# Cross-attention and feed-forward block: three output weights in the projection weights' buffers, attention results fetched one head group ahead, and the first pair's last output group recorded inside the second pair

## The chip, the core and the metric

The kernel runs on one core of one Trainium2 chip. The metric is the device time of one execution in microseconds (us); of each kernel several executions are timed, and the median stands for it. Beside these, one execution was taken with the hardware profiler; every view of the profile comes from that one. Engines are called as in the profile: PE (TensorE), DVE (VectorE), ACT (ScalarE), POOL (GpSimd), SP (SyncE, which here only issues transfers).

## What is computed

Eight sequences `x` of 128 tokens by 512 features, eight contexts `ctx` of the same size, float32 throughout. Cut to what matters, the reference is

```
n   = layernorm(x)
h   = rmsnorm(n) * ln_weight
q   = h @ w_q.T;  k = ctx @ w_k.T;  v = ctx @ w_v.T        # 32 heads of 128
p   = softmax(q k.T + position_bias, where mask else -inf)  # per head, 128 x 128
att = p @ v                                                # 128 x 4096
x1  = x + n + att @ w_out.T                                # 4096 -> 512
f   = layernorm(x1)
out = x1 + ((silu(f @ Wg.T * ag) * (f @ Wu.T * au)) @ Wd.T) * ad   # 512 -> 1376 -> 512
```

The change lies in the part from `p` to `x1`.

## The kernel before

**Products in seven.** The large products (q, k, v, output, gate and up) are cut into two by two blocks and made from seven block products instead of eight, with sums of blocks before and after. The sums of a weight's blocks are four instructions on POOL (`sums_a`, L191, for the projections; `sums_b`, L199, for the output weights). The sums of the attention results are four on DVE (`sums_a`, called in `attended`, L450). Their outputs go to a tile of sums beside the weight or result, and one block of the operand itself is overwritten.

**Stages.** The 32 heads are eight groups of four (g), the eight sequences four pairs (i).
1. Keys and values of group 0, the first norms, then the queries of all groups, which are stored in DRAM.
2. The loop over g (L491), inside it the loop over eight sequences b (L510). For each b the scores of four heads (`probabilities`, L292), softmax, a transposition by way of DRAM (`transpose_p`, L331: a DVE transpose, one store `turned`, four loads `pT`), and, three steps later (`advance(3)`), the product with v (`attend`, L353), whose result goes to DRAM (`att[g][i]`). Between these steps the keys and values of group g + 1 are projected (`kv`, L371), three or four block products a step, each for one half of the outputs.
3. The output projection. `out_products(i, order, banks)` (L462) is a generator: for each group g it loads `att[g][i]` as tile `a` (L452), makes the sums S_a on DVE, and records 28 matmuls (fourteen in the source, each executed as two) into four PSUM banks. Each pair needs all eight groups. The first pair's banks are the projections' own (`first_banks`), so its groups are interleaved with the loop of g = 7, where no projection is left: one `next(first_out)` after each of b = 0 to 6, and the last after `advance(0)` (L528). Then come the residual and second norm of pair 0 (`residual`, L536, `norm2`, L557), and the pairs 1 to 3 with all their products (L582 on).
4. Feed-forward, in the end the down projection (L712).

**Output weights.** `load_wo(g)` (L443) loads 1 MB and records four POOL sums into T_o. Weights 0 and 1 have buffers of their own (`wosA`) and are loaded at g = 1 and 2. Weights 2 to 6 get buffers (`wosB`, five) in the place of the context tile `toks`, which the projections read to their end: the pools `toks`, `spool` (sums of projection weights, two buffers) and `wpool` (projection weights, three buffers) are closed together at g = 7 (L502). Weight 7 uses activation buffers and is loaded after the loop.

**What sets the order.** The source gives each instruction its engine and its priority by the place where it is recorded. A scheduler then orders each engine's instructions, assigns buffers and adds the waits. On the chip each engine's queue is taken in that order: an instruction that waits holds up all that stand behind it, also the transfers on SP, which loads `wo`, `a`, `q`, `pT` and stores `turned` and `att`. POOL has, besides the weight sums, the sum of bias and mask for each step (L296), which the softmax needs; three such tiles `s` are in turn. Scores have two PSUM banks, attends two, and `acts` holds eighteen tiles for k, v, q, a and S_a together.

Of the kernel before, what the change touches and what calls it, by code (L numbers as in the profile page):

```python
# [9 lines left out]
F32 = mybir.dt.float32  # L10
# [4 lines left out]
PSUM = bass.MemoryType.PSUM  # L15

P = 128
# [8 lines left out]
def xattn_ffn_kernel(  # L26
# [20 lines left out]
    B, S, D = x.shape  # L47
    H = pbias.shape[0]
    INTER = wgT.shape[1]
    T = B * S  # L50
    DC = D // P
    GH = 4
    NG = H // GH
# [5 lines left out]
    HC = DC // 2  # L59
    HW = GW // 2  # L60
    ADD, SUB = ALU.add, ALU.subtract

    def pools(stack):
        def pool(name, bufs=1, **kw):
            return stack.enter_context(tc.tile_pool(name=name, bufs=bufs, **kw))
        return pool
# [6 lines left out]
    work = pool("work", 2, side="right", reuse_waits="tile")  # L73
    small = pool("small", 4, side="right", reuse_waits="tile")

    proj, rows, attn = ExitStack(), ExitStack(), ExitStack()
    toks = pools(proj)("toks", reuse_waits="tile")
    spool = pools(proj)("spool", 2, reuse_waits="tile")
    wpool = pools(proj)("wpool", 3, reuse_waits="tile")
    hpool = pools(rows)("hpool", side="right", reuse_waits="tile")  # L80
    ps_mm, ps_tp, ps = (pools(attn)(f"ps{n}", 2, space=PSUM) for n in ("mm", "tp", "at"))

    def load_w(name, src):
        t = wpool.tile([P, DC, GW], F32, tag="w", name=name)
# [341 lines left out]
    outp = ExitStack()  # L426
# [3 lines left out]
    def load_wo(g):  # L430
        src = woT[bass.ts(g, GW), :].rearrange("(c p) n -> p c n", p=P)
        if g == NG - 1:
            up, dn, t12, t4 = (
                acts.tile([P, 2, D], F32, tag="a", name=f"wo{g}_{k}") for k in range(4)
            )
            nc.sync.dma_start(up, src[:, :HC])
            nc.sync.dma_start(dn, src[:, HC:])
            t1, t2, t4 = (
                t.rearrange("p (c n) -> p c n", c=HC) for t in (t12[:, 0], t12[:, 1], t4[:, 0])
            )  # L440
        else:
            w = wos.tile([P, GH, D], F32, tag="w", name=f"wo{g}")
            nc.sync.dma_start(w, src)  # L443
            t = wos.tile([P, 3, HC, HW], F32, tag="T", name=f"T_o{g}")
            up, dn, t1, t2, t4 = w[:, :HC], w[:, HC:], t[:, 0], t[:, 1], t[:, 2]
        wo_t[g] = sums_b(
            nc.gpsimd, up[:, :, :HW], up[:, :, HW:], dn[:, :, :HW], dn[:, :, HW:], t1, t2, t4
        )

    def attended(g, i):  # L450
        a = acts.tile([P, 2, GH, S], F32, tag="a", name=f"a_{g}_{i}")
        nc.sync.dma_start(a, att[g][i])  # L452
        s = acts.tile([P, 3, HC, S], F32, tag="a", name=f"S_a{g}_{i}")
        return sums_a(
            nc.vector, a[:, 0, :HC], a[:, 0, HC:], a[:, 1, :HC], a[:, 1, HC:],
            s[:, 0], s[:, 1], s[:, 2],
        )

    def by_product(banks):
        return {n: banks[k // 2][:, k % 2, :] for k, n in enumerate((1, 2, 6, 7, 4, 5, 3))}  # L460

    def out_products(i, order, banks):  # L462

        m = by_product(banks)
        for g in order:
            sa = attended(g, i)
            for k, n in enumerate((1, 2, 6, 7, 4, 5, 3)):
                for c in range(HC):
                    nc.tensor.matmul(  # L469
                        m[n], sa[n][:, c, :], wo_t[g][n][:, c, :],  # L470
                        start=(g == order[0] and c == 0 and k % 2 == 0),
                        stop=(g == order[-1] and c == HC - 1), skip_group_check=True,
                    )
            yield


    def load_bias(g):
# [13 lines left out]
    for g in range(NG):  # L491
        kT, v = kvs.pop(g)
        pb = biases.pop(g)
        if g + 1 < NG:
            biases[g + 1] = load_bias(g + 1)
        if g + 2 < NG:
            kv_w[g + 2] = load_kv(g + 2)
        products = kv(g + 1, kvs) if g + 1 < NG else iter(())
        if g in (1, 2):
            load_wo(g - 1)  # L500
        if g == NG - 1:
            proj.close()  # L502
            wos = pools(outp)("wosB", NG - 3, reuse_waits="tile")

            first_banks = [
                pl.tile([P, 2, HW], F32, tag=tag, name=f"m{k}_0")
                for k, (pl, tag) in enumerate(((ps_mm, "mm"), (ps_mm, "mm"), (ps_tp, "pt"), (ps_tp, "pt")))
            ]
            first_out = out_products(0, list(range(NG)), first_banks)
        for b in range(B):  # L510
            if b % 2 == 0:
                qT = ahead.pop((g, b // 2))
                at = todo.index((g, b // 2)) + 2
                if at < len(todo):
                    ahead[todo[at]] = load_queries(*todo[at])
            p = probabilities(g, b, qT, kT, pb)
            pend.append((g, b, transpose_p(g, b, p), v))
            advance(3)
            for _ in range(4 if b % 2 else 3):
                next(products, None)  # L520
            if g == NG - 1:
                if b < NG - 3:
                    load_wo(b + 2)
                if b < NG - 1:
                    next(first_out)
    load_wo(NG - 1)
    advance(0)
    next(first_out)  # L528
    attn.close()


# [4 lines left out]
    def residual(i, xs, m, banks):  # L536
        r1, r2 = xs[:, 0, :], xs[:, 1, :]
        u = work.tile([P, 2, HW], F32, tag="s", name=f"u_{i}", bufs=3)
        w = work.tile([P, HW], F32, tag="s", name=f"u7_{i}", bufs=3)
        nc.scalar.copy(u[:, 0], m[1])  # L540
        nc.vector.tensor_tensor(u[:, 1], u[:, 0], m[6], ADD)
        nc.vector.tensor_tensor(w, u[:, 1], m[7], ADD)
        nc.vector.tensor_tensor(r1[:, :HW], r1[:, :HW], m[2], ADD)
        nc.gpsimd.tensor_tensor(r1[:, :HW], r1[:, :HW], u[:, 0], ADD)
        nc.vector.tensor_tensor(r1[:, HW:], r1[:, HW:], m[5], ADD)
        nc.vector.tensor_tensor(r1[:, HW:], r1[:, HW:], m[3], ADD)
        nc.gpsimd.tensor_tensor(r1[:, HW:], r1[:, HW:], u[:, 1], ADD)
        nc.vector.tensor_tensor(r2, r2, banks[2][:].rearrange("p a n -> p (a n)"), ADD)
        nc.vector.tensor_tensor(
            r2.rearrange("p (a n) -> p a n", a=2), r2.rearrange("p (a n) -> p a n", a=2),  # L550
            w.unsqueeze(1).to_broadcast([P, 2, HW]), ADD,
        )
# [4 lines left out]
    def norm2(i, xs):  # L557
        for k in range(2):
            st = small.tile([P, nc.vector.BN_STATS_DIM], F32, tag="st", name=f"st2_{i}_{k}")
            moments(mv2, 2 * i + k, st, xs[:, k, :])  # L560
        pair = slice(2 * i, 2 * i + 2)
        rstd_of(rs2[:, pair], mv2[:, pair, 1], 1.0)
        ys = []
        for b in (2 * i, 2 * i + 1):
            y = work.tile([P, D], F32, tag="aT", name=f"y2_{b}")
            nc.vector.tensor_scalar(
                y, xs[:, b % 2, :], mv2[:, b, 0:1], rs2[:, b : b + 1], ALU.subtract, ALU.mult
            )
            ys.append((b, y))
        return ys  # L570

    def norm2_T(b, y):
        th, cols = b * S // 512, bass.ds(b * S % 512, S)
        if (0, th) not in h2:
            for f in range(2):
                h2[f, th] = acts.tile([P, HC, 512], F32, tag="a", name=f"h2_{f}_{th}")
        tp = transposed(y, ps.tile([P, DC, P], F32, tag="tp", name="tp2", bufs=1))
        nc.vector.tensor_copy(h2[0, th][:, :, cols], tp[:, :HC])
        nc.scalar.copy(h2[1, th][:, :, cols], tp[:, HC:])

    x1, ys, banks = [], [], first_banks
    for i in range(B // 2):  # L582
        last = i + 1 == B // 2
        order = [2, 3, 4, 5, 6, 7, 0, 1] if last else list(range(NG))
        if i:
            banks = [ps.tile([P, 2, HW], F32, tag="m", name=f"m{k}_{i}") for k in range(4)]
            for n, _ in enumerate(out_products(i, order, banks)):
                if n == 2:
                    for y in ys:
                        norm2_T(*y)  # L590
        m = by_product(banks)
        x1.append(acts.tile([P, 2, D], F32, tag="a", name=f"x1_{i}"))
        for k in range(2):
            b = 2 * i + k
            nc.sync.dma_start(x1[i][:, k, :], x[b])
            nc.scalar.activation(
                x1[i][:, k, :], x1[i][:, k, :], AF.Identity,
                bias=res_bias[:, b : b + 1], scale=res_scale[:, b : b + 1],
            )
        if last:  # L600
            outp.close()
        else:
            residual(i, x1[i], m, banks)
            ys = norm2(i, x1[i])
# [157 lines left out]
```

## Time and profile before

| | us |
|---|---|
| time, median of 3 executions (lowest, highest) | 1152.94 (1151.9, 1153.74) |
| time of the profiled execution | 1155.07 |
| span of its profile | 1153.3 |
| first score of group 7, on PE | 698.43 |
| fourth group of matmuls after the gap at 777.01 ends | 802.90 |
| output products L469: `wo` with `a`, mean of one matmul | 0.389 |
| landing of `wo` (1 MB), least, median, most | 6.2, 7.5, 11.5 |
| landing of `a` (0.5 MB), least, median, most | 3.1, 3.4, 9.8 |
| landing of `turned` in 700:770, least, median, most | 2.2, 4.8, 8.6 |

A row of the timeline reads: start in us from the span's start, duration in us, engine, line, operation, output <- inputs, number; in brackets how long the engine stood idle before it and what released it. "PE" are matmuls, "PEld" the loads of their stationary operand; "SPq" are issues of transfers, whose duration is that of the issue and not of the transfer. Landing is the time from issue to the end of the transfer.

### The profile page before, as it was taken

The numbers are of one execution on the slowest core, as the hardware profiler recorded it, in microseconds if no ns is written. First come the engines' busy times: TensorE is split into PE (matmuls) and PEld (weight loads), VectorE is DVE, ScalarE is ACT, GpSimd is POOL, SyncE is SP. The second block draws the span as 40 slices with busy tenths as digits, with TensorE's granted clock in tenths as the row PEclk, the third lists the DMA queues.
The fourth block names the chain that finished last, engine by engine and source line by source line (L and its number), as shares of the span: only waits on it lengthen the run. The fifth ranks groups of instructions, "written<-read, shape, count | busy, mean of one in ns | idle before, by whom it ended". The sixth has DMA issues, their size and how long they took to land.

```text
span 1153.3 us, 12296 instructions
## 1 busy us (share of the span) xinstructions
PE 1116.4 (97%) x4286; PEld 729.4 (63%) x4286; DVE 501.0 (43%) x937; ACT 317.4 (28%) x889; POOL 307.3 (27%) x255
## 2 busy tenths in 40 slices
PE   6899999999999999999999999689999999999998
PEld 3564444445867677686858688578888864444445
DVE  4541111116555556555555557724433253433311
ACT  2521112223444344434344433301000022222000
POOL 5331221116333333333223314530000034330000
PEclk9999999999999999999999999899999999999999
DMA  9114423257646465555554446864222322110000
GB/s 281 43 37 149 178 110 110 109 204 252 187 138 200 145 192 162 176 181 174 184 172 148 135 146 199 256 217 170 92 92 80 116 99 73 36 37 1 15 31 28
DMA packets 117534, 154.38 MB, mean 134 GB/s; under 512 B 12033, under 2 KB 71681, under 8 KB 117473
## 3 DMA queue, kind: packets, MB, share of 16 engines
q1 hardware_dynamic: 114784, 149.93, 40.4%
q10 hardware_dynamic: 2192, 2.10, 0.6%
q0 software_dynamic: 496, 1.58, 0.4%
q8 instruction: 34, 0.56, 0.2%
q14 instruction: 28, 0.22, 0.1%
HBM read 101.14 MB, written 52.43 MB: 133 GB/s over the span
## 4 chain that ended last, share of the span: by engine, by line
PE 90%; DVE 4%; DMA 4%; issue 1%; ACT 1%; SPq 0%; ACTq 0%; DVEq 0%
PE mm_q L261 17%; PE mm_v L279 16%; PE mm_k L261 15%; PE m L469 15%; PE mm_f L688 9%; PE dn L712 7%; PE sc L301 4%; PE av L357 4%; DMA turned<-tt 1%; DMA wk<-in_wkT_dram 1%; DVE sg L640 1%; DMA a<-att 1%; DVE act L643 1%; PE tp L152 1%; PE up L654 1%
## 5 line engine op out<-in xcount | busy, mean ns | idle before, releaser
L296 POOL TENSOR_TENSOR s<-pb,mneg 128x512 f32<-128x512 f32 x64 | 81.2, 1269 | 290.7 <-DVE tt L334 234.0
L261 PE MATMUL mm_k<-ctx_sb,wk 128*128 128x512 f32 x256 | 117.4, 603 | 7.5 <-DMA wk<-in_wkT_dram 4.4
L279 PE MATMUL mm_v<-wv,ctx_sb 128*128 128x256 f32 x512 | 115.9, 379 | 1.3 <-DMA wv<-in_wvT_dram 1.3
L261 PE MATMUL mm_q<-hT,wq 128*128 128x512 f32 x256 | 112.5, 592 | 0.0
L469 PE MATMUL m<-wo,a 128*128 128x256 f32 x400 | 100.6, 389 | 9.6 <-DMA a<-att 9.1
L311 ACT ACTIVATE s<-s,nmx 128x128 f32<-128x128 f32 x256 | 99.5, 390 | 37.4 <-DVE nmx L308 37.4
L279 PEld LDWEIGHTS mm_v<-wv,ctx_sb 128*128 128x128 f32 x512 | 95.1, 190 | 14.8 <-DMA wv<-in_wvT_dram 2.1
L362 ACT COPY aT<-av 128x512 f32<-128x512 f32 x64 | 37.5, 586 | 202.9 <-PE av L357 98.5
L261 PE MATMUL mm_k<-ctx_sb,S_k 128*128 128x512 f32 x192 | 87.8, 605 | 4.4 <-DVE k L240 4.0
L469 PEld LDWEIGHTS m<-wo,a 128*128 128x128 f32 x400 | 77.1, 196 | 21.2 <-DMA a<-att 9.5
L261 PEld LDWEIGHTS mm_q<-hT,wq 128*128 128x128 f32 x256 | 48.6, 190 | 60.8 <-issue 60.7
L279 PE MATMUL mm_v<-S_v,ctx_sb 128*128 128x256 f32 x384 | 86.4, 381 | 0.0
L261 PEld LDWEIGHTS mm_k<-ctx_sb,wk 128*128 128x128 f32 x256 | 46.9, 193 | 60.4 <-issue 45.2
L261 PE MATMUL mm_q<-hT,S_q 128*128 128x512 f32 x192 | 85.0, 592 | 0.0
L304 DVE TENSOR_TENSOR s<-sc,s 128x512 f32<-128x512 f32 x64 | 44.2, 690 | 86.0 <-PE sc L301 82.9
L301 PEld LDWEIGHTS sc<-k,q 128*128 128x128 f32 x512 | 67.4, 194 | 17.9 <-issue 13.4
L279 PEld LDWEIGHTS mm_v<-S_v,ctx_sb 128*128 128x128 f32 x384 | 71.7, 190 | 10.6 <-DVE v L251 1.5
L712 PE MATMUL dn<-wd,act 128*128 128x512 f32 (+3 forms) x198 | 75.8, 545 | 0.0
L251 DVE TENSOR_TENSOR q<-q,mm_q 128x512 f32<-128x512 f32 x32 | 22.0, 688 | 114.8 <-PE mm_q L261 114.8
L301 PE MATMUL sc<-k,q 128*128 128x128 f32 x512 | 68.1, 277 | 2.8 <-DMA q<-queries 2.8
L357 PE MATMUL av<-pT,v 128*128 128x128 f32 x512 | 67.9, 277 | 0.0
L261 PEld LDWEIGHTS mm_k<-ctx_sb,S_k 128*128 128x128 f32 x192 | 35.6, 193 | 48.6 <-issue 35.7
(156 smaller groups left out, 1494.3 us busy)
## 6 DMA issues: line engine op xcount, KB each, us to landing
queries<-q SPq DMA_DIRECT2D x32, 512.0 KB, 3.8
q<-queries SPq DMA_DIRECT2D x32, 512.0 KB, 4.5
turned<-tt SPq DMA_DIRECT2D x64, 256.0 KB, 2.2
pT<-turned SPq DMA_DIRECT2D x256, 64.0 KB, 2.5
att<-aT SPq DMA_DIRECT2D x64, 256.0 KB, 2.3
a<-att SPq DMA_DIRECT2D x32, 512.0 KB, 3.4
wq<-in_wqT_dram SPq DMA_DIRECT2D x8, 1024.0 KB, 5.6
wk<-in_wkT_dram SPq DMA_DIRECT2D x7, 1024.0 KB, 6.2
```

The source lines that it names most:

```text
L251: nc.vector.tensor_tensor(part(r, c, t), part(r, c, t), m[t], ADD)
L261: nc.tensor.matmul(out, w[i][:, c, bass.ts(t, P)], src[i][:, c, :], start=(first and c == 0), stop=(c == HC - 1), skip_group_check=True,)
L279: nc.tensor.matmul(out[:, bass.ts(k, HW)], src[i][:, c, bass.ts(2 * t + k, S)], w[i][:, c, :], start=(first and k == 0 and c == 0), stop=( ...
L296: nc.gpsimd.tensor_tensor(s, pb, mneg[:, b : b + 1, :].to_broadcast([P, GH, S]), ALU.add)
L301: nc.tensor.matmul(sc[:, j, :], qT[:, j, bass.ts(b % 2, S)], kT[j][:, cols], start=True, stop=True)
L304: nc.vector.tensor_tensor(s, sc, s, ALU.add)
L311: nc.scalar.activation(s[:, j, :], s[:, j, :], AF.Exp, bias=nmx[:, j : j + 1], accum_out=sm[:, j : j + 1],)
L357: nc.tensor.matmul(av[:, j, :], v[b // 2][:, b % 2, bass.ts(j, P)], pT[:, :, j, :], start=True, stop=True,)
L362: nc.scalar.copy(aT, av)
L469: nc.tensor.matmul(m[n], sa[n][:, c, :], wo_t[g][n][:, c, :], start=(g == order[0] and c == 0 and k % 2 == 0), stop=(g == order[-1] and c ...
L688: nc.tensor.matmul(out, ws[t][n][:, c, :], h2_t[n][:, c, :], start=(first and c == 0), stop=(c == HC - 1), skip_group_check=True,)
L712: nc.tensor.matmul(o, act[ic][:m, bass.ts(b, S)], wd[:m, ic, cols], start=(n == 0), stop=(n == NI - 1),)
```

## The change

The pools of projection weights and their sums are put below the context tile and stay open to the end of the output projection; the sums get three buffers instead of two. Weights 2, 3 and 4 take their buffers; weight 2 is recorded at g = 6, weights 3 to 6 in the steps b = 0 to 3 of g = 7, one step earlier than before. Of the context tile's place two buffers are used (weights 5 and 6). `out_products` records the load and the sums of the next group ahead of the matmuls of this one. (The argument `ahead=False` is not used by any call.) The first pair's last group and its residual are recorded after the second group of the second pair, and its second norm's transposes after the fifth. The PSUM pools are opened in another order.

```diff
-    proj, rows, attn = ExitStack(), ExitStack(), ExitStack()
+    proj, rows, attn, wts = ExitStack(), ExitStack(), ExitStack(), ExitStack()
+    spool = pools(wts)("spool", 3, reuse_waits="tile")
+    wpool = pools(wts)("wpool", 3, reuse_waits="tile")
     toks = pools(proj)("toks", reuse_waits="tile")
-    spool = pools(proj)("spool", 2, reuse_waits="tile")
-    wpool = pools(proj)("wpool", 3, reuse_waits="tile")
     hpool = pools(rows)("hpool", side="right", reuse_waits="tile")
-    ps_mm, ps_tp, ps = (pools(attn)(f"ps{n}", 2, space=PSUM) for n in ("mm", "tp", "at"))
+    ps, ps_mm, ps_tp = (pools(attn)(f"ps{n}", 2, space=PSUM) for n in ("at", "mm", "tp"))
...
         else:
-            w = wos.tile([P, GH, D], F32, tag="w", name=f"wo{g}")
+            held = g in (2, 3, 4)
+            w = (wpool if held else wos).tile([P, GH, D], F32, tag="w", name=f"wo{g}")
             nc.sync.dma_start(w, src)
-            t = wos.tile([P, 3, HC, HW], F32, tag="T", name=f"T_o{g}")
+            t = (spool if held else wos).tile(
+                [P, 3, HC, HW], F32, tag="S" if held else "T", name=f"T_o{g}"
+            )
...
-    def out_products(i, order, banks):
+    def out_products(i, order, banks, ahead=True):
 
         m = by_product(banks)
-        for g in order:
-            sa = attended(g, i)
+        coming = attended(order[0], i)
+        for n, g in enumerate(order):
+            sa = coming
+            if n + 1 < NG and ahead:
+                coming = attended(order[n + 1], i)
             for k, n in enumerate((1, 2, 6, 7, 4, 5, 3)):
...
             yield
+            if n + 1 < NG and not ahead:
+                coming = attended(order[n + 1], i)
...
         if g in (1, 2):
             load_wo(g - 1)
+        if g == NG - 2:
+            load_wo(2)
         if g == NG - 1:
             proj.close()
-            wos = pools(outp)("wosB", NG - 3, reuse_waits="tile")
+            wos = pools(outp)("wosB", 2, reuse_waits="tile")
...
             if g == NG - 1:
-                if b < NG - 3:
-                    load_wo(b + 2)
+                if b < NG - 4:
+                    load_wo(b + 3)
                 if b < NG - 1:
                     next(first_out)
     load_wo(NG - 1)
     advance(0)
-    next(first_out)
     attn.close()
...
+    ys = []
+    for i in range(1, B // 2):
+        last = i + 1 == B // 2
+        order = [2, 3, 4, 5, 6, 7, 0, 1] if last else list(range(NG))
+        banks = [ps.tile([P, 2, HW], F32, tag="m", name=f"m{k}_{i}") for k in range(4)]
+        for n, _ in enumerate(out_products(i, order, banks)):
+            if i == 1 and n == 1:
+
+                next(first_out)
+                first_residual(0)
+                residual(0, x1[0], by_product(first_banks), first_banks)
+                ys = norm2(0, x1[0])
+            if n == (4 if i == 1 else 2):
+                for y in ys:
+                    norm2_T(*y)
+        m = by_product(banks)
+        first_residual(i)
         if last:
             outp.close()
+            wts.close()
```

`first_residual(i)` is the loading of x and the scaled sum of x and its first norm that stood in the loop before.

## The prediction

> **What bounds the kernel now.** I read the engine shares first, then the chain that ended last, then TensorE's timeline in the stretch that the change touches.
>
> ```profile
> PE 1116.4 (97%) x4286; PEld 729.4 (63%) x4286; DVE 501.0 (43%) x937; ACT 317.4 (28%) x889; POOL 307.3 (27%) x255
> PE 90%; DVE 4%; DMA 4%; issue 1%; ACT 1%; SPq 0%; ACTq 0%; DVEq 0%
> ```
>
> TensorE is busy nearly everywhere and is 90% of the chain. A change that leaves its matmuls alone can win only where TensorE stands still. Windows of 5 us show one such place, the last head group (the loop with g = 7) and the hand-over after it; columns are PE, PEld, DVE, ACT, POOL, then granted clock, DMA share, GB/s:
>
> ```profile
> 710.00:715.00 5.00, 5.00 (x29) 4.51 (x28) 3.21 (x4) 1.65 (x8) 4.43 (x5) 1.00 0.38 80
> 720.00:725.00 5.00, 2.62 (x12) 2.65 (x13) 4.97 (x10) 3.34 (x17) 1.27 (x1) 0.69 0.90 234
> 730.00:735.00 5.00, 3.23 (x8) 2.52 (x8) 2.94 (x4) 1.65 (x8) 4.92 (x4) 0.50 0.43 134
> 775.00:780.00 5.00, 2.99 (x7) 2.45 (x8) 1.52 (x4) 0.00 (x0) 0.00 (x0) 0.66 0.97 288
> ```
>
> The timeline names what TensorE waits for (brackets), and the slow matmuls after a gap:
>
> ```profile
> 722.38 2.05 PE L301 MATMUL sc<-k,q 128*128 128x128 f32 x8 [2.77 <-DMA q<-queries]
> 731.76 3.78 PE L469 MATMUL m<-wo,a 128*128 128x256 f32 x8 [5.05 <-DMA a<-att]
> 737.54 1.10 PE L469 MATMUL m<-T_o,S_a 128*128 128x256 f32 x4 [2.00 <-DVE S_a L194]
> 777.01 3.44 PE L469 MATMUL m<-wo,a 128*128 128x256 f32 x8 [4.03 <-DMA a<-att]
> ```
>
> Sizing the loss: from the first score of group 7 (698.43) to the start of the second pair's output products there are 8 scores and 11 attends of 0.89 us and 8 output groups of 6.05 us (the chain: "700.38 6.05 PE m L469 x28"), 65.4 us of work. The chain has 112 matmuls from 777.01 in 25.89 us; four groups are 24.2, so 1.7 is warming up and the second pair starts at 784.75. That took 86.3 us: **20.9 us are lost**. This is the ceiling of the gain. Afterwards TensorE is full to the end (920:940 and 940:960 show 20.00 of 20).
>
> Why it stalls is in the timelines of SyncE's queue and of GpSimd, and in the chain (start, us, what):
>
> ```profile
> 698.62 0.38 SPq L443 DMA_DIRECT2D wo<-in_woT_dram  x1
> 722.36 0.49 SPq L452 DMA_DIRECT2D a<-att  x1
> ```
>
> ```profile
> 729.89 1.27 POOL L201 TENSOR_TENSOR T_o<-wo 128x512 f32<-128x512 f32 x1 [3.40 <-DMA wo<-in_woT_dram]
> ```
>
> ```profile
> 725.10 7.34 DMA turned<-tt
> ```
>
> wo2 cannot start before 698.6, when the context tile is dead. Five 1 MB weights then share the DMA engines with the turned probabilities (7 to 8 us each instead of 2.2), and the attention result of group 2 is issued only at 722.36, in order.
>
> **What the Trainium skill says.** (1) "SBUF — State Buffer", Who interferes with whom: a VectorE instruction with two SBUF inputs contends with a GpSimd instruction that reads SBUF. The trace agrees: S_a takes 0.42 us, but 1.37 to 1.49 while T_o runs (744.06 to 748.2); L304, with one PSUM input, stays 0.69. (2) "TensorE: Matmul & The Clock Gate", What's actually happening: idle of about 3.4 us halves the clock. The trace shows 3.78 for 1.89 after 5.05 us, already 2.05 for 1.05 after 2.77, nothing after 2.00. A gap over 2.7 us therefore costs 1.5 more. (3) "DMA: Bandwidth & Descriptors", Issuing engines are not separate DMA queues: all queues share 16 engines and interleave, so a small transfer issued behind 1 MB is slow, as the 7.34 above.
>
> **The change part by part**, from the order of the built program.
>
> *Three weights early.* wo2 takes wv6's buffer, free after 626.99; wo3 takes wk7's, free at 658.3; wo4 wv7's, free at 689.7. Each stands on SP behind a turned store (626.39, 657.75, 689.14) and ahead of that block's pT loads (628.42, 660.44, 691.18), so the wait holds nothing up. The median landing of all weight loads of this matrix is 7.1 us. Their 12 GpSimd sums (1.27 us each, 15 us) go to a queue that is idle some 70% there: 0 us as long as wo2 lands in time. T_o2's first sum stands before wk7's, so wk7's second sum ends at about 634.1 + 6 x 1.45 = 642.8; TensorE needs it at 646.23: cover 3.4 us. The worst landing seen, 11.5, gives 638.5 and 647.2: 1 us lost. In group 7, 3 MB leave the DMA engines.
>
> *The third sum buffer* lets the projections' sums run earlier. wq0's four now stand at 31 to 36 us, beside first-norm work that TensorE waits for (3.12 us, released by ACT L143, at 34.34). Two y of 0.53 us may become 1.2 (25.85: 2.53 for two): cost 0 to 1.5, I take 0.5. wk2's sums delay s_0_3 by some 2 us, 7 ahead of its score at 281.2: 0.
>
> *Fetching a group ahead and the new order.* TensorE's order is now: group 2 before score 3, then scores 3 to 6 and the first of score 7, groups 3 to 6, rest of score 7, attends 4 to 6, group 7, attend 7, second pair. I walk it with the durations above.
> - a0 is issued after turned 6_7 (about 696.8) and lands at 700.3 to 701.3; group 0 starts at 701. T_o4 runs at 698.6 to 703.8, so S_a0's second sum ends at 703.9, not 702.6: 1.3 lost. Group 1 runs 709.5 to 715.6.
> - wo5 is issued after the turned store of block 0 (709) and lands at 716; a2, behind it, at about 719, where score 2 and attend 6_7 end at 717.4: 1.6 lost, and 1.2 on S_a2 beside T_o5. Group 2 ends at 726.2.
> - wo6 waits for wo5's semaphore and lands at 723.5. GpSimd, in order: T_o5 to 721.5, s_7_4, T_o6 to 728.7, s_7_5 to 730. VectorE adds it at 731.8; only then is the score buffer free for score 7's first part. Queued behind that matmul are groups 3 to 6. It and a3 (below) let group 3 start at 732.5; six scores and attends of 0.89 and 0.22 would have been over at 731.8: 0.7 lost.
> - Groups 3 to 6 need a3 (SP behind turned 7_2 at 727.5, landing 732 to 733), then one per 6.9 us; a4 to a6 land in 3.4 to 4.9: 0 lost, since 7 us of matmuls cover them. 732.5 + 4 x 6.05 + two attends 1.78 + score 7's rest 0.67 = 759.2, with 0.5 for small waits: 759.7.
> - Tail: softmax of block 7: sums of S_a7 first (760.3), then 0.69 + 0.70 + 0.17 + exp 1.7 + 0.35 + 1.6 (beside T_o7) + 0.70, turned 2.2, four issues 1.75, landing 2.5 to 3.1, some 0.3 of gaps: 773.3. Attends 4 to 6 and group 7 (waiting about 1 for wo7) end at 769.5. Attend 7 waits 3.8 us, plus 1.5 warming up. The second pair starts at 773.3 + 0.9 + 1.5 = 775.7.
>
> *Moving the first pair's last group.* In TensorE's built order it still stands before the second pair; only residual and norm of pair 0 move behind S_a of the second pair. x[b]'s two loads move behind three a loads on SP. Needed by the transposes after group 4, some 25 us later: 0. The second pair's banks are those of scores and attends; the last is free when aT_7_7 is copied (0.59) under 5 us of matmuls: 0. FFN weights now wait for wo4's last use instead of wo6's (902 against 916.4): earlier, 0.
>
> Sum: 784.75 - 775.7 = 9.0 us, less 0.5: **8.5 us**. The profiled span 1153.3 becomes 1144.8 and its run 1155.07 becomes 1146.6; that run is 2.1 above the median 1152.94, so the median becomes **1144.4**.
>
> **Rivals.**
> A. *Waits in the middle vanish.* If T_o5, T_o6 and S_a2 do not delay (1.3 + 1.6 + 1.2 + 0.7 + 0.5 = 5.3), only the tail is left: gain 13.8, 1139.1. For: DMA is lighter by 3 MB. Against: the GpSimd queue is in order and wo5, wo6 still start after 698.6.
> B. *GpSimd binds.* If wo5 and wo6 each land after 11.5 us, s_7_5 comes at 738.4 and group 3 at 739.7, 7 us later: gain 1.5, 1151.5. For: 8.7 us was seen for wo4 at 721.16. Against: three fewer weights compete.
> C. *Slower: a ring through VectorE, SyncE and DMA.* S_a3 stands ahead of block 3's transpose on VectorE, whose store stands ahead of a4 on SP, S_a4 ahead of block 5's, and so on. Each turn is a landing plus some 3 us, against 6.9 of matmuls. It decides from a landing of 4 us; at the worst seen, 9.8, four turns lose 4 x 5.9 = 23.6, so 8.5 - 23.6 = 15 slower: 1168; at 7 us, 4 x 3.1 = 12.4, 4 slower: 1157. For: 9.8 us happened in this stretch. Against: it happened with wo loads in flight; later ones took 4.3 to 4.9.
> D. *The early sums cost more* than 0.5 and wo2 is late: 1.5 + 1 - 0.5 = 2 less gain, 1146.4: within the forecast's own range.
>
> **How the numbers follow.** Forecast with D 0.57 (own range 1141 to 1148), A 0.18, B 0.17, C 0.08 (1157). The time is the likeliest one's. The range from 1138.5 to 1151.5 takes in A and B. A measurement can tell 0.2%, 2.3 us, from no change: forecast, A and half of B are faster, 0.84; half of B is the same, 0.08; C is slower, 0.08.
>
> **What would show it.** Right: L443's loads (L444 now) at about 627, 658 and 690; L475 group 2 before score 3; no 5 us wait at group 3; a 3 to 4 us wait at attend 7; second pair near 775. Wrong: group 3 after 738, waits of L475 on S_a from group to group, or mm_k at 646 waiting for GpSimd.

## The result, and the profile after

The changed kernel took 1155.25 us (median of 20 executions, 1150.66 to 1157.97), the kernel before, timed beside it, 1153.88. The ratio on record is 1.0004, 95% interval 0.9997 to 1.0011 (the quotient of the two medians is 1.0012): no change that can be measured, where 1144.4 us was forecast. The profiled execution took 1153.51 us, its span is 1151.7.

The engine shares and the chain of the page show no new limit: TensorE is as full as before (97%), and DVE has gained two points of the chain.

```profile
PE 1117.8 (97%) x4286; PEld 728.8 (63%) x4286; DVE 504.2 (44%) x937; ACT 316.9 (28%) x889; POOL 307.3 (27%) x255
PE 87%; DVE 6%; DMA 4%; ACT 1%; issue 1%; POOL 1%; SPq 0%; ACTq 0%; DVEq 0%; POOLq 0%
```

The windows of 5 us show where the difference lies (columns as before: PE, PEld, DVE, ACT, POOL, clock, DMA share, GB/s). In the windows up to 735 TensorE is busy for at least 4.00 of 5.00 us. After 775 comes a hole that the kernel before did not have: in 780:785 one matmul starts, and the clock is low around it (0.59, 0.76, 0.56).

```profile
710.00:715.00 5.00, 5.00 (x24) 4.39 (x24) 3.15 (x6) 2.24 (x9) 2.04 (x2) 1.00 1.03 340
720.00:725.00 5.00, 4.98 (x26) 4.47 (x27) 2.46 (x7) 1.65 (x8) 1.47 (x2) 1.00 0.76 204
730.00:735.00 5.00, 4.00 (x18) 3.23 (x19) 5.00 (x12) 1.47 (x8) 1.29 (x1) 1.00 0.39 128
775.00:780.00 5.00, 4.21 (x12) 2.95 (x11) 1.52 (x4) 0.59 (x1) 0.00 (x0) 0.59 0.54 154
780.00:785.00 5.00, 0.36 (x1) 0.39 (x2) 3.39 (x9) 2.73 (x3) 0.82 (x2) 0.76 0.98 363
785.00:790.00 5.00, 5.00 (x14) 4.00 (x14) 4.35 (x14) 0.28 (x2) 1.01 (x1) 0.56 0.15 62
```

TensorE's timeline names it. (m0 to m3 are the four banks of a pair, a2 and S_a2 the attention result of head group 2 and its sums, attend 7 that of the last sequence.)

```profile
701.74 1.97 PE L475 MATMUL m<-wo,a 128*128 128x256 f32 x8 [0.73 <-DMA a<-att]
730.72 0.49 PE L301 MATMUL sc<-k,q 128*128 128x128 f32 x2 [0.76 <-DVE s L304]
773.75 2.05 PE L357 MATMUL av<-pT,v 128*128 128x128 f32 x8 [4.71 <-DMA pT<-turned]
775.59 3.62 PE L475 MATMUL m<-wo,a 128*128 128x256 f32 x8
784.64 2.04 PE L475 MATMUL m<-T_o,S_a 128*128 128x256 f32 x4 [5.43 <-DVE x L557]
786.48 1.91 PE L475 MATMUL m<-wo,a 128*128 128x256 f32 x4
788.18 1.63 PE L475 MATMUL m<-T_o,a 128*128 128x256 f32 x4
791.37 1.89 PE L475 MATMUL m<-wo,a 128*128 128x256 f32 x8
```

In the kernel before, TensorE was full here (20.00 of 20), and the second pair's first two groups started at 784.60 (784.75 in the prediction's reckoning) and 790.65:

```profile
780.00:800.00 20.00, 20.00 (x94) 17.60 (x94) 10.17 (x27) 3.26 (x5) 1.95 (x2) 1.00 0.55 197
784.60 1.89 PE L469 MATMUL m<-wo,a 128*128 128x256 f32 x8
790.65 1.89 PE L469 MATMUL m<-wo,a 128*128 128x256 f32 x8
```

The 5 us wait ahead of a group (731.76 before) is gone, and the second pair starts at 775.59 instead of 784.60. But after eight matmuls TensorE stands 5.43 us, released by L557, the residual of the *first* pair: `r2 += banks[2]`. Its second group starts at 791.37, where it was 790.65. The whole 9 us are given back within one group: 5.43 us of standing, 3.62 - 1.89 = 1.7 and (2.04 + 1.91 + 1.63) - 3 x 1.03 = 2.5 us of slow matmuls, 9.7 together.

Why a matmul of pair 1 waits for a sum of pair 0 is seen in the built program's PSUM banks. Pair 0 holds banks 4, 5, 6, 7 (m0 to m3), pair 1 got 0, 6, 5, 4: its second bank, m1, is number 6, the one that L557 reads. The new sums would overwrite what L557 still has to read, so they wait for it. Besides, the Trainium skill ("PSUM — Partial Sum Buffer", PSUM bank collisions raise a hardware error) asks for PSUM to be guarded by bank and quadrant, or in the simple version by bank, since two engines must not meet in one; the trace shows the length of this wait, 5.43 us. And L557 is late for the reason that the other queues show (DVE, ScalarE, SyncE):

```profile
781.57 0.42 DVE L193 TENSOR_TENSOR S_a<-a 128x256 f32<-128x256 f32 x1 [4.30 <-DMA a<-att]
...
783.10 0.42 DVE L552 TENSOR_TENSOR x<-x,m 128x256 f32<-128x256 f32 x1
...
783.80 0.69 DVE L557 TENSOR_TENSOR x<-x,m 128x512 f32<-128x512 f32 x1
...
782.25 1.52 ACT L597 ACTIVATE x<-x,res_bias,res_scale 128x512 f32<-128x512 f32 x2 [5.79 <-DMA x<-in_x_dram]
...
776.49 0.34 SPq L363 DMA_DIRECT2D att<-aT  x1
776.92 0.38 SPq L455 DMA_DIRECT2D a<-att  x1
777.40 0.89 SPq L596 DMA_DIRECT2D x<-in_x_dram  x2
```

On SP, a2 of pair 1 and then x stand behind the store of attend 7's result (L363, 776.49). On DVE the residual stands behind S_a2, whose operand was issued at 776.92 and landed 4.62 us later. Four sums of 1.5 us together, L552, L554 and L557: 784.5. The scaled x is no earlier: ScalarE ends it at 782.25 + 1.52 = 783.77, just before L557 starts.

Two theories were put to the test. *Bank*: the stall is the wait for banks which pair 0's residual still has to read, and its time is set by that residual's place on DVE and SP. *Fixed end*: pair 1 could not have run sooner anyway (attention results, x, weights of the feed-forward), so the stall would only move.

### The profile page after: what moved, and what is told of

It is laid out like the page before. It is cut to its first block, busy times and chain, and to the rows that moved or that the text cites. A ratio compares the mean times of both kernels' runs of the same rounds, so it can differ in the third digit from the quotient of the medians.

```text
span 1151.7 us, 12291 instructions
## 1 busy us (share of the span) xinstructions
PE 1117.8 (97%) x4286; PEld 728.8 (63%) x4286; DVE 504.2 (44%) x937; ACT 316.9 (28%) x889; POOL 307.3 (27%) x255
## 4 chain that ended last, share of the span: by engine, by line
PE 87%; DVE 6%; DMA 4%; ACT 1%; issue 1%; POOL 1%; SPq 0%; ACTq 0%; DVEq 0%; POOLq 0%
PE mm_q L261 17%; PE m L475 15%; PE mm_k L261 15%; PE mm_v L279 15%; PE mm_f L708 9%; PE dn L732 7%; PE sc L301 5%; PE av L357 4%; DMA a<-att 1%; DMA pT<-turned 1%; DMA wv<-in_wvT_dram 1%; DVE sg L660 1%; DVE act L663 1%; PE tp L152 1%; PE up L674 1%
## 5 line engine op out<-in xcount | busy, mean ns | idle before, releaser
L357 PEld LDWEIGHTS av<-pT,v 128*128 128x128 f32 x512 | 63.3, 194 | 5.3 <-issue 5.1
```

Of the source, the lines that this page charges most:

```text
L357: nc.tensor.matmul(av[:, j, :], v[b // 2][:, b % 2, bass.ts(j, P)], pT[:, :, j, :], start=True, stop=True,)
```

## The experiments

Each was timed beside the kernel before, with 4 to 22 executions. As the start of the program scatters (in the profiles the first score of group 7 lies between 698.0 and 701.4 us, also among kernels with the same code up to there), the profiles are compared by one stretch: from that score to the first matmul of the third pair.

| kernel | median us | ratio to before, 95% interval | stretch, us | against before |
|---|---|---|---|---|
| before | 1154.5 to 1154.8 | | 834.97 - 698.43 = 136.5 | |
| after | 1155.25 | 1.0004 (0.9997 to 1.0011) | 834.55 - 698.39 = 136.2 | -0.4 |
| e1 banks apart | 1143.48 | 0.9897 (0.9882 to 0.9911) | 826.34 - 701.32 = 125.0 | -11.5 |
| e2 x early | 1144.43 | 0.9908 (0.9891 to 0.9925) | 822.59 - 698.02 = 124.6 | -12.0 |
| e3 move undone | 1148.02 | 0.9935 (0.9922 to 0.9948) | 828.42 - 700.29 = 128.1 | -8.4 |
| e4 old pool order | 1156.41 | 1.0010 (0.9999 to 1.0021) | 837.49 - 700.78 = 136.7 | +0.2 |
| e5 fetch ahead alone | 1151.64 | 0.9978 (0.9965 to 0.9991) | 833.07 - 698.53 = 134.5 | -2.0 |
| e6 weights alone | 1157.66 | 1.0023 (1.0012 to 1.0034) | 836.35 - 701.44 = 134.9 | -1.6 |
| e7 move alone | 1159.90 | 1.0036 (1.0022 to 1.0050) | 840.09 - 700.21 = 139.9 | +3.3 |
| e8 both cures | 1144.23 | 0.9907 (0.9892 to 0.9921) | 826.35 - 700.42 = 125.9 | -10.6 |
| e9 move later | 1155.74 | 1.0012 (1.0000 to 1.0024) | 833.64 - 698.20 = 135.4 | -1.1 |
| e10 x early, 19 buffers | 1142.23 | 0.9892 (0.9872 to 0.9912) | 826.60 - 701.03 = 125.6 | -11.0 |
| e11 banks apart, 19 buffers | 1138.72 | 0.9862 (0.9842 to 0.9882) | 819.76 - 701.14 = 118.6 | -17.9 |
| e12 score early, 19 buffers | 1146.03 | 0.9920 (0.9902 to 0.9939) | 825.22 - 701.02 = 124.2 | -12.3 |

**e1: other banks, nothing moved.** Pairs 1 and 3 take the banks of scores and attends, pair 2 those of the projections; the transposes of the second norm go to these pools too (not shown here).

```diff
-        banks = [ps.tile([P, 2, HW], F32, tag="m", name=f"m{k}_{i}") for k in range(4)]
+        banks = [
+            pl.tile([P, 2, HW], F32, tag=tag, name=f"m{k}_{i}")
+            for k, (pl, tag) in enumerate(
+                ((ps_tp, "pt"), (ps_tp, "pt"), (ps_mm, "mm"), (ps_mm, "mm")) if i == 2
+                else ((ps, "av"), (ps, "av"), (ps, "sc"), (ps, "sc"))
+            )
+        ]
...
-    attn.close()
...
+            attn.close()
+            ps = psO = pool("psO", 7, space=PSUM, reuse_waits="tile")
```

> The changed kernel with other PSUM banks: the pairs 1 and 3 take the banks of scores and attends, pair 2 those of the projections, so no pair writes a bank that the residual of the pair before has still to read. Nothing else is moved; the x loads and the residual of pair 0 stay where the change put them. Theory (bank): the new stall of 5.43 us ahead of m1 of the second pair (784.64) is a wait for a bank that L557 still has to read, and its price is 5.4 plus about 2.4 of slow matmuls, 8 us; also, two of the second pair's products no longer wait for attend 7's bank and may fill 2.6 us of the 4.7 us wait ahead of attend 7: 8 to 11 us under the changed kernel, ratio to the kernel before 0.991 to 0.993. Rival (fixed end): what follows cannot start earlier (attention results or weights of the feed-forward arrive no sooner), the stall moves to the next group: within 2 us of the changed kernel, ratio 0.999 to 1.001.

Measured: 0.9897, some 12 us under the changed kernel, a little beyond the upper end. TensorE's and DVE's timelines:

```profile
774.43 1.38 PE L475 MATMUL m<-T_o,a 128*128 128x256 f32 x4 [2.14 <-DMA a<-att]
775.61 1.91 PE L475 MATMUL m<-T_o,S_a 128*128 128x256 f32 x4
777.31 1.66 PE L475 MATMUL m<-wo,S_a 128*128 128x256 f32 x4
778.81 1.05 PE L357 MATMUL av<-pT,v 128*128 128x128 f32 x8
779.71 1.89 PE L475 MATMUL m<-wo,a 128*128 128x256 f32 x8
781.43 1.03 PE L475 MATMUL m<-T_o,S_a 128*128 128x256 f32 x4
...
787.86 0.69 DVE L556 TENSOR_TENSOR x<-x,m 128x512 f32<-128x512 f32 x1
```

The residual's reading (L556 here, L557 above) is at 787.86, as late as in the changed kernel, and m1 starts at 781.43 without a bracket: no wait. So the residual's lateness costs nothing when its bank is not wanted. Besides, twelve matmuls of pair 1 now run ahead of attend 7, whose wait is gone; so e1 gains in two places.

**e2: same banks, x earlier.**

```diff
                 if b < NG - 1:
                     next(first_out)
+                if b == 6:
+                    first_residual(0)
...
-                first_residual(0)
```

> The changed kernel with one edit: the two loads of x and their scaled sum for pair 0 are recorded in the last step b = 6 of group 7. Banks are as in the changed kernel (5, 6 and 4 are shared by pair 0 and pair 1), but the residual now stands ahead of S_a1 and S_a2 of the second pair on DVE. Theory (bank): what made the bank late is the place of the residual in DVE's queue, behind S_a2 whose operand landed at 781.6, and x that landed at 782.3; now L557 is over soon after group 7 ends (768 to 771) and the stall is gone: 7 to 8 us under the changed kernel, ratio 0.993. Rival (fixed end): 0 to 2 us under it, ratio 0.999 to 1.001.

Measured: 0.9908, 11 us under the changed kernel, more than expected. The banks are shared as before, but DVE reads the last one at 773.26, ahead of S_a1, and m1 follows at 775.09 without a wait:

```profile
764.83 1.13 PE L475 MATMUL m<-wo,a 128*128 128x256 f32 x4 [2.33 <-DMA wo<-in_woT_dram]
772.40 1.13 PE L357 MATMUL av<-pT,v 128*128 128x128 f32 x8
773.37 1.89 PE L475 MATMUL m<-wo,a 128*128 128x256 f32 x8
775.09 1.03 PE L475 MATMUL m<-T_o,S_a 128*128 128x256 f32 x4
...
773.26 0.68 DVE L571 TENSOR_TENSOR x<-x,m 128x512 f32<-128x512 f32 x1
```

From the second pair's start to the third's, e2 takes 822.59 - 773.37 = 49.2 us and the changed kernel 834.55 - 775.59 = 59.0: 9.7 less, as much as was counted above. Some 2 us more are won ahead of the second pair, where attend 7 no longer waits (4.71 in the changed kernel) and 2.33 for `wo` appear.

Either cure alone takes away the whole stall: *bank* stands, *fixed end* falls.

**e3: the move undone.** The last group, residual and norm of pair 0 stand ahead of pair 1 again; the rest of the change stays.

```diff
     advance(0)
+    next(first_out)
...
+    first_residual(0)
+    residual(0, x1[0], by_product(first_banks), first_banks)
+    ys = norm2(0, x1[0])
     for i in range(1, B // 2):
...
```

> The changed kernel with its third part undone: the first pair's last group, residual and norm are recorded ahead of the second pair, as in the kernel before; early weights, fetch ahead and the order of the PSUM pools stay. In the built order x is loaded just ahead of the last pT, and the residual stands on DVE ahead of S_a0 of the second pair. Theory (bank): x lands at about 774, residual 776 to 779, S_a0 until 781, m1 of the second pair starts at about 780.5 instead of 784.6: 3 to 4 us under the changed kernel, ratio 0.997. Rival (fixed end): 0 to 1 us, ratio 1.000.

Measured: 0.9935, 7 us under the changed kernel, twice what was expected: S_a0 came sooner than reckoned, and m1 did not wait at all.

```profile
776.03 2.04 PE L357 MATMUL av<-pT,v 128*128 128x128 f32 x8 [5.29 <-DMA pT<-turned]
777.87 3.21 PE L475 MATMUL m<-wo,a 128*128 128x256 f32 x8
780.92 1.03 PE L475 MATMUL m<-T_o,S_a 128*128 128x256 f32 x4
```

So two of the three parts (with the new pool order) gain 7.5 us, and the third, meant only as a move, takes them back.

**e4: the PSUM pools in the old order** (`"mm", "tp", "at"`), all else as changed. Pairs 0 and 1 then share bank 0 alone.

> The changed kernel with the PSUM pools opened in the order of the kernel before. The pairs 0 and 1 then share one bank instead of three, but it is the one that the second pair's first product goes to. Theory (bank): the stall moves from m1 to m0 of the second pair; it ends at about 783 (L552, behind S_a2 and x) instead of 784, and 2 us of matmuls come behind it instead of ahead: within 1.5 us of the changed kernel, ratio 0.999 to 1.002. Rival (the pool order alone is at fault): the stall is gone, 7 to 8 us under the changed kernel, ratio 0.993.

Measured: 1.0010. The stall is at pair 1's first product now, and longer, with slow matmuls behind it (3.78 for 1.89):

```profile
775.60 2.04 PE L357 MATMUL av<-pT,v 128*128 128x128 f32 x8 [4.81 <-DMA pT<-turned]
785.42 3.78 PE L475 MATMUL m<-wo,a 128*128 128x256 f32 x8 [7.77 <-DVE x L552]
```

It is not the number of shared banks that counts, but when the first of them is wanted and when it has been read.

**e5, e6, e7: one part alone, on the kernel before.** e5 has the fetch ahead, e6 the early weights with their buffers, e7 the move.

> The kernel before with one part of the change: attention results are loaded and summed one group ahead. Weights 2 to 6 are still loaded in group 7, the pair 0 is closed before pair 1, the PSUM order is the old one. Theory (each part by itself shortens the gaps of the tail, the move alone lengthens one): the 5.05 us wait for a2 and the 4.03 us wait for a7 go in part, but five weights still share the DMA engines: 3 to 5 us faster than before, ratio 0.996 to 0.997. Rival (only all parts together bring it): 0.999 to 1.001.

> The kernel before with one part of the change: weights 2, 3 and 4 in the buffers of the projection weights, three buffers of sums. No fetch ahead, pair 0 closed before pair 1, old PSUM order. Theory: transfers of group 7 compete with three weights less, so a2 lands sooner (the 5.05 us wait shrinks to 1 to 2, its 1.9 us of slow matmuls go), the wait ahead of group 7 stays: 3 to 5 us faster, ratio 0.996 to 0.997; together with the fetch ahead (the kernel with the move undone) 0.9935 was measured. Rival (weights alone bring nothing, since the attention result stays in the same place in the queue): 0.999 to 1.001.

> The kernel before with one part of the change: the first pair's last group, the residual and the norm are recorded after the second group of the second pair. Everything else as before; PSUM banks 0 (pair 0 and pair 1) are shared, and the first product of pair 1 waits for the residual. Theory (bank): in the kernel before the residual reads bank 0 under the last 20 matmuls of group 7, at no cost; here its read stands on DVE behind S_a0 and S_a1 of pair 1 and behind x, which is issued after a1: a stall of 1.5 to 4 us at the first product of pair 1 and 1.5 us of slow matmuls if it is over 2.7: 2 to 5 us slower, ratio 1.002 to 1.004. Rival (the move costs nothing, or the fault lies in the fetch ahead): 0.999 to 1.001.

Measured: 0.9978, 1.0023 and 1.0036. In e5 the wait for a2 shrinks to 1.27 us, but S_a stands late at the next group. On DVE its first two sums start at 735.54 and 738.67, among steps of the softmax, and take 1.48 and 1.08 us, beside sums on POOL (0.42 alone). The wait for a7 stays:

```profile
718.96 1.99 PE L472 MATMUL m<-wo,a 128*128 128x256 f32 x8 [1.27 <-DMA a<-att]
739.90 2.05 PE L472 MATMUL m<-T_o,S_a 128*128 128x256 f32 x4 [5.94 <-DVE S_a L194]
781.43 3.75 PE L472 MATMUL m<-wo,a 128*128 128x256 f32 x8 [4.29 <-DMA a<-att]
```

In e6 a loss was measured where a gain was expected. Its stretch is 1.6 us shorter than before; a 4.61 us wait on S_a takes the place of the 5.05 for a2. But the part behind the stretch is 1.9 us longer (1156.6 - 836.35 = 320.2 against 1153.3 - 834.97 = 318.3). Of the four loads of feed-forward weights on POOL the first was issued at 890.70 before; in e6 all are issued from 903.31 on. Four feed-forward matmuls that stand early in e6's order wait 1.60 us for the first:

```profile
744.66 2.05 PE L472 MATMUL m<-T_o,S_a 128*128 128x256 f32 x4 [4.61 <-DVE S_a L194]
907.49 1.96 PE L660 MATMUL gp<-h,wg 128*96 128x512 f32 x4 [1.60 <-DMA wg<-in_wgT_dram]
```

The first score of group 7 was 3 us later in its profile. Whether that start belongs to the early weights or to the scatter named above is open. Together the two parts give 0.9935 (e3, with the new pool order), far more than the sum of each alone.

e7 is slower by as much as expected, but not for the reason given. TensorE's timeline:

```profile
781.62 3.75 PE L469 MATMUL m<-wo,a 128*128 128x256 f32 x8 [8.95 <-DMA a<-att]
```

This is pair 0's group 7, waiting for a7: without the fetch ahead, the move puts the load of a7 behind a0 and a1 of pair 1 on SP; in the kernel before it stood ahead of them, and the wait was 4.03. The bank costs nothing there. The sign came out right, the mechanism of the expectation did not.

**e8: both cures together** (e1 and e2).

> The changed kernel with both cures of the earlier runs: banks apart and x loaded in the last step of group 7. Theory (bank): each cure already takes the whole stall away, so both together bring no more than the 2.6 us of products that run ahead of attend 7: within 2 us of the better of the two, ratio 0.988 to 0.991. Rival (the two take away different stalls): they add up, ratio 0.982.

Measured: 0.9907. The two do not add up; they take away the same stall.

**e9: the residual one group later** (`n == 2` for `n == 1`).

> The changed kernel with the first pair's last group and its residual recorded one group later in the second pair (after the third instead of the second group). On DVE the residual then stands behind S_a3 too, and x is issued behind a3 on SP; banks as in the changed kernel. Theory (the stall lasts until the residual has read the bank): its end moves with S_a3 and x, by some 1.7 us of sums and up to 1 us of landing: 1.5 to 3 us over the changed kernel, ratio 1.002 to 1.003. Rival (the stall is set by something else, such as the landing of a2): within 0.7 us of the changed kernel, ratio 1.000.

Measured: 1.0012, not to be told from the changed kernel, where 1.002 to 1.003 was expected. As a test of the residual's place it failed: S_a2 began 2 us sooner (779.61), which made up for the four added sums. It shows something else, though:

```profile
772.92 1.13 PE L357 MATMUL av<-pT,v 128*128 128x128 f32 x8 [3.30 <-DMA pT<-turned]
784.03 2.05 PE L475 MATMUL m<-T_o,S_a 128*128 128x256 f32 x4 [8.26 <-DVE x L557]
...
783.21 0.68 DVE L557 TENSOR_TENSOR x<-x,m 128x512 f32<-128x512 f32 x1
```

Attend 7 ended 1.75 us earlier than in the changed kernel (772.92 + 1.13 against 773.75 + 2.05), the stall grew from 5.43 to 8.26 us, and it ended only 0.6 us sooner: its end is fixed by L557, and time won ahead of it is only spent standing.

**e10, e11, e12: the next limit.** Nineteen activation buffers (`acts`) instead of eighteen, on e2, on e1, and on e2 with group 6 recorded behind block 7.

> The kernel with x early (changed kernel, x of pair 0 loaded at b = 6) with nineteen activation buffers instead of eighteen. There the second half of weight 7 was issued at 760.82, 4.3 us behind the first, for want of a buffer, and group 7 waited 2.33 us for it. With one more buffer the built order moves group 3 ahead of score 6 and the loads come earlier. Theory (bank, and buffers as the next limit of this tail): 1 to 4 us under the kernel with x early, ratio 0.987 to 0.990. Rival (the tail is now set by the softmax chain of block 7): no change, ratio 0.991.

> The kernel with banks apart (x and residual where the change put them) with nineteen activation buffers. In the built order four products of pair 1 now stand ahead of attend 7, 5 us of matmuls, so its wait for the turned probabilities should be hidden, if a0 and a1 of pair 1 land in time. Theory (bank, buffers next): 1 to 4 us under the kernel with banks apart, ratio 0.986 to 0.989. Rival: what stood ahead of attend 7 waits for a0 and a1 instead: no change, ratio 0.990.

> The kernel with x early and nineteen buffers, and with the first pair's group 6 recorded behind block 7 instead of ahead of it, so that the last scores are made a group earlier and their softmax runs beside group 6; attend 7 then stands ahead of group 7, and a7 is loaded late. Theory: the 4 to 5 us wait of attend 7 shrinks, but group 7 waits for a7: 0 to 3 us under the kernel with x early, ratio 0.988 to 0.991. Rival: the late a7 costs as much as the softmax saves or more: ratio 0.991 to 0.994.

Measured: 0.9892, 0.9862, 0.9920. e10 cannot be told from e2. e12 gains nothing and lies in the range of its rival: group 7 waits 1.82 us for a7 there. e11 is the fastest kernel of this study, 16 us under the kernel before. In its tail one wait above 0.5 us is left after 740: six products of pair 1 (24 matmuls as executed; four were expected) run ahead of attend 7, which no longer waits.

```profile
737.53 1.99 PE L475 MATMUL m<-wo,a 128*128 128x256 f32 x8 [1.78 <-DMA a<-att]
739.92 1.10 PE L475 MATMUL m<-T_o,S_a 128*128 128x256 f32 x4 [0.40 <-DVE S_a L194]
769.11 1.13 PE L475 MATMUL m<-T_o,a 128*128 128x256 f32 x4 [1.10 <-DMA a<-att]
```

The extra buffer also changes the order of the groups and scores; how much each brings was not separated.

## Why the prediction was wrong

Step by step:

- **The early weights** came as reckoned: their loads stand at 626.33, 658.40 and 689.82 (627, 658 and 690 forecast), and the projection of keys waited at 640.76 only 0.44 us, for ScalarE. The 0.5 us for early sums at the start can't be told from the scatter: TensorE's first query matmul was at 67.71, against 69.05 before.
- **The walk through group 7** was right within some 1.5 us at its marks on TensorE: group 0 at 701.74 (701), group 3 behind the score at 730.72 (732.5), attend 7 after a wait of 4.71 (3.8), second pair at 775.59 (775.7). One term was undersized: warming up after attend 7's wait was charged 1.5 us and took 2.7, 1.0 of it in attend 7 (2.05 for 1.05) and 1.7 in the second pair's first products (3.62 for 1.89). And "7 to 8 us each" for the transfers of `turned` was true of the slowest only; their median in this stretch was 4.8 before.
- **The step that failed** is in the third part: "The second pair's banks are those of scores and attends; the last is free when aT_7_7 is copied (0.59) under 5 us of matmuls: 0." Three of the four were pair 0's banks. With it fell the step ahead, which asked only who reads the moved residual's result ("Needed by the transposes after group 4, some 25 us later: 0"), not who waits for the banks that the residual frees: TensorE, 2 us after the second pair's start. In the place of these two zeros the runs show 11 to 12 us (changed kernel against e2 and e1), of which 9.7 are seen in the profile as standing and slow matmuls; in e2 the rest lies ahead of the second pair, where attend 7 no longer waits.
- **The sum without that step** was of the right size. 8.5 us were forecast; 7.5 us were measured with the move taken out (e3: 0.9935, 0.9922 to 0.9948), 10.6 with the move kept and x early (e2).
- **The feed-forward's weights**, the third zero of that part, cost nothing here: TensorE waits for none of them. But "earlier" holds for three of the four loads only; the first, issued at 890.70 before, comes at 901.51.
- **The rivals**: A and B did not come about (group 3 was at 731, not 738). C, the slower one, is a ring through the same three queues, but no such wait from group to group appeared, the stall was a single one in another place, and no slower kernel was measured.

That the 9 us were gained and then given back is shown by e1 and e2, which keep all three parts. Open are the rest of e6's loss and the scatter of the start.

## What to carry to other kernels

A step that is moved later holds its inputs longer: for each buffer and bank that it reads, look up in the built program who writes there next, and put that writer's time beside the new end of the step. Where a wait ends on an instruction deep in an in-order queue, follow that queue back to its slowest input; loading 0.5 MB of x a few steps earlier cured here what looked like a lack of PSUM banks. Parts of a change on one stretch do not add up (-2.5, +2.7 and +4.2 us alone, +0.5 together, -7.5 without the third), so walk them together and try them apart.

## What was not expected of the hardware

The slow matmuls after a gap cost more than the 1.5 us that were charged, and the gap need not be long. After 5.43 us TensorE ran slow from 784.64 to about 789, costing 2.5 us. In e1 a gap of 2.14 us was followed by 1.38, 1.91 and 1.66 for 1.03 each, while in e7 one of 2.48 us cost almost nothing:

```profile
729.49 1.99 PE L469 MATMUL m<-wo,a 128*128 128x256 f32 x8 [2.48 <-DMA a<-att]
```

The Trainium skill ("TensorE: Matmul & The Clock Gate", What's actually happening) says that the clock watches a window that runs freely, with some 3.4 us of idle time before the slow state and some 3.4 us of slow time after it. That the length of the last gap alone does not decide fits a window that runs freely. But slow matmuls after 2.14 us come at less idle time than it states, and the slow stretch of more than 4 us is longer.
